# Two-layer graph network: slot rows of the convolutions go from one SBUF tile straight into another, in three parts of sources, with 14 slots per pair

## The chip, the cores and the metric

The kernel runs on one core of a Trainium2 chip. The metric is the device time of one execution in microseconds (us). The kernel before took 7372.2 us in the median of 9 runs (7339.61 to 7401.35). A profile is one more execution, taken by the hardware profiler: TensorE (PE, with its weight loads PEld), VectorE (DVE), ScalarE (ACT), GpSimd (POOL), and the DMA queues that SyncE (SP) and POOL issue on.

## The reference, cut to what matters

A graph of 12500 nodes with 128 features and 200000 edges, sorted by destination. First an attention layer over the edges, then three graph convolutions with a batch norm after each. The change touches the convolutions only (and the sorted lists that are made for them):

```python
def _gcn_conv(x, W, b, src, dst, norm, num_nodes):
    h = x @ W
    msg = h[src] * norm[:, None]
    out = jax.ops.segment_sum(msg, dst, num_segments=num_nodes)
    return out + b
...
h = _gcn_conv(x, W1, b1, src, dst, norm, n)
h = _batch_norm(jax.nn.relu(h), g1, beta1)
h = _gcn_conv(h, W2, b2, src, dst, norm, n)
h = _batch_norm(jax.nn.relu(h), g2, beta2)
h = _gcn_conv(h, W3, b3, src, dst, norm, n)
return _batch_norm(h, g3, beta3)
```

So each convolution adds, for every edge, the 128 floats of the source's row onto the destination's row.

## The kernel before

**Tiles and pairs.** Destinations are cut into 106 tiles of 118 nodes (`TN`, `NTT`), sources into 98 groups of 128 nodes (`NS`). A pair is one tile and one group. For each pair the kernel keeps `SB` = 13 slots, each with one edge; edges beyond those go to a list of up to `OV` = 768 per tile. The lists are made while the attention layer runs (`place_edges`): `dlS` holds each slot's destination within its tile, `gi_d` each slot's source within its group, `srcO` the rows of the listed edges.

**A convolution** (`conv_slots`, run three times) holds all source rows in SBUF (`hs`) and works in 12 blocks (`NBK`) of 9 tiles (`TB`).

- `take(b, m)` makes the rows of all slots of a block. For seven batches of 14 groups it loads the slots' sources (`gi`, SP's queue), compares them with the partition number on VectorE (`go`, L1221), multiplies that one-hot matrix by the group's rows on TensorE (`gp`, L1224), copies the result to `stage` on ScalarE (L1226) and writes it to a DRAM tile `m` (L1228).
- `reduce(b, m)` adds a block's rows up, tile by tile. It reads the tile's 1274 slot rows back from `m` (`mr`, L1245, three transfers per tile), gathers the 768 listed rows with six indirect transfers on POOL (`rows`, L148), makes the one-hot matrix of the destinations on VectorE (`oh`, L1249, 16 x 118 columns in one instruction) and runs on TensorE one matmul for the tile's own rows (L1159), ten over `mr` (L1253) and six over `rows` (L1255), all into one PSUM tile `zp`. Every matmul is float32 and appears as two instructions.
- `finish` closes a group of three tiles: it loads `tg` and `db` ahead of their matmuls, multiplies by `db` (L1163) and hands over to `use1`, `use2` or `use3`.

The reduction of block b-1 is written between the batches of `take(b)`:

```python
for g, _ in enumerate(take(b, taken)):
    while done < g * TB * SG // (NS - SG):
        next(tiles, None)
        done += 1
```

Each engine runs its instructions in the order in which the scheduler of the language put them, and SP and POOL issue their transfers in such an order too. Buffers: `stage` 2, `mr` 3, `rows` (pool `ga`) 5, `gi` 3, `m` 3 in DRAM.

Of the kernel before, what the change touches and what calls it, by code (L numbers as in the profile page):

```python
# [8 lines left out]
FP = mybir.dt.float32  # L9
# [8 lines left out]
P = 128  # L18
# [19 lines left out]
SB = 13  # L38
OV = 768
JO = OV // P  # L40
TB = P // SB
GN = 3
SG = 14
# [5 lines left out]
def tile_gnn(ctx: ExitStack, tc: tile.TileContext, x, src, dst, ea, wqkvT, weT, w1, w2, w3, par, out):  # L49
# [20 lines left out]
    assert TB % GN == 0  # L70
    RC = -(-SL // P)
    LP, LR = divmod(SL, RC)
    assert NS % SG == 0 and 112 < LP < P and LR and RC * P <= WE and NS * P * P < LATE and TN < P
    NBK = -(-NTT // TB)

    def groups(n, g):
        return [(a, min(g, n - a)) for a in range(0, n, g)]

# [15 lines left out]
    gi_d = dram.tile([NBK, NS // SG, TB, SG * SB], U8, name="gi_d")  # L94
# [563 lines left out]
    def fast():  # L658
# [6 lines left out]
        srcO = fc.tile([P, NTT, JO], I32, name="srcO")  # L665
        pars = fc.tile([P, 12], FP, name="pars")
# [12 lines left out]

        def place_edges(rt, ps):  # L680
# [10 lines left out]
            def turned(a, n, o, copy):  # L691

                av = a[:, :n * P].rearrange("t (p c) -> t c p", c=n)
                for c, m in groups(n, 4):
                    tp = ps.tile([P, 4, P], FP, name="et_p")
                    for i in range(m):
                        nc.tensor.transpose(tp[:, i, :NTT], av[:, c + i, :], ident[:NTT, :NTT])
                    copy(o[:, :, c:c + m].rearrange("p t c -> p c t"), tp[:, :m, :NTT])
# [102 lines left out]
            turned(x1, JO, dlS[:, :, RC:], nc.scalar.copy)  # L801
# [8 lines left out]
            turned(y1, JO, srcO, nc.vector.tensor_copy)  # L810
# [34 lines left out]
            for b in range(10, -1, -1):  # L845
# [7 lines left out]
                if sh < SL:  # L853
# [10 lines left out]
            nc.vector.tensor_scalar(mov, cur, P - 1, None, op0=ALU.bitwise_and)  # L864
            yield
            nc.vector.tensor_copy(A[turn][:, :SL].rearrange("t (k s) -> t k s", s=NS),
                                  mov.rearrange("t (s k) -> t k s", k=SB))
            turned(A[turn], RC, dlS[:, :, :RC], nc.scalar.copy)
# [5 lines left out]
            for b in range(NBK):  # L874
                tn = min(TB, NTT - b * TB)
                nc.sync.dma_start(gi_d[b, :, :tn, :].rearrange("g t k -> t g k"),
                                  sl[b * TB:b * TB + tn, :].rearrange("t (g k) -> t g k", g=NS // SG))
            if NTT % TB:
                none = rt.tile([NS // SG, (TB - NTT % TB) * SG * SB], U8, name="none")
                yield  # L880
                nc.vector.memset(none, 255)
                nc.sync.dma_start(gi_d[NBK - 1, :, NTT % TB:, :].rearrange("g t k -> g (t k)"), none)

# [266 lines left out]
        def finish(wk, table, t0, n, zp, use, ps, add):  # L1150

            tg = wk.tile([TN, GN, D], FP, name="tg")
            for a, b in ((0, 112), (112, TN)):
                nc.sync.dma_start(tg[a:b, :n, :], rows118(table, t0, n, a, b))
            db = wk.tile([P, GN * TN], FP, name="db")
            nc.sync.dma_start(db[:, :n * TN],
                              dinv_d[t0 * TN:(t0 + n) * TN].unsqueeze(0).to_broadcast([P, n * TN]))
            for i in range(n):
                nc.tensor.matmul(zp[:, i, :], tg[:, i, :], ident[:TN, :TN], start=True, stop=False)  # L1159
                add(i)  # L1160
                yield
# [5 lines left out]
        def conv_rows(table, use):  # L1167

            with ExitStack() as s:
# [8 lines left out]
                for t0, n in groups(NTT, GN):  # L1178
                    zp = ps.tile([P, GN, TN], FP, name="zp")

                    def add(i):
# [7 lines left out]

                    for _ in finish(wk, table, t0, n, zp, use, ps, add):  # L1190
                        pass

        def conv_slots(table, use):
# [3 lines left out]
            with ExitStack() as s:  # L1197
                tb = s.enter_context(tc.tile_pool(name="tb", bufs=1, space=PSUM))
                nums = tb.tile([P, TN], FP, name="nums")
                nc.vector.tensor_copy(nums, iota_f[:, :TN])  # L1200
                blocks = s.enter_context(tc.tile_pool(name="blocks", bufs=3, space=DRAM))
                gy = s.enter_context(tc.tile_pool(name="gy", bufs=3))
                gx = s.enter_context(tc.tile_pool(name="gx", bufs=3))
                sg = s.enter_context(tc.tile_pool(name="sg", bufs=2))
                mt = s.enter_context(tc.tile_pool(name="mt", bufs=3))
                ga = s.enter_context(tc.tile_pool(name="ga", bufs=5))
                wk = s.enter_context(tc.tile_pool(name="wk", bufs=2))
                ps = s.enter_context(tc.tile_pool(name="ps", bufs=2, space=PSUM))
                TS = TB * SB

                def take(b, m):
                    for g in range(NS // SG):
                        stage = sg.tile([TS, SG, D], FP, name="stage")
                        gi = gy.tile([P, TB, SG * SB], U8, name="gi")
                        nc.sync.dma_start(gi.rearrange("p t k -> p (t k)"),
                                          gi_d[b, g].rearrange("t k -> (t k)").unsqueeze(0)
                                          .to_broadcast([P, TS * SG]))
                        gv = gi.rearrange("p t (s k) -> p s t k", k=SB)
                        for a, n in groups(SG, 4):
                            go = gx.tile([P, 4, TB, SB], FP, name="go")  # L1220
                            nc.vector.tensor_scalar(go[:, :n], gv[:, a:a + n], iota_q, None, op0=ALU.is_equal)  # L1221
                            gp = ps.tile([TS, 4, D], FP, name="gp")
                            for i in range(n):
                                nc.tensor.matmul(gp[:, i, :], go[:, i].rearrange("p t k -> p (t k)"),  # L1224
                                                 hs[:, g * SG + a + i, :], start=True, stop=True)
                            nc.scalar.copy(stage[:, a:a + n, :], gp[:, :n, :])  # L1226
                        for x, y in ((0, 112), (112, TS)):
                            nc.sync.dma_start(m[x:y, g * SG:(g + 1) * SG, :], stage[x:y])  # L1228
                        yield

                def reduce(b, m):
                    for t0 in range(b * TB, min(NTT, (b + 1) * TB), GN):
                        n = min(GN, NTT - t0)
                        zp = ps.tile([P, GN, TN], FP, name="zp")

                        def add(i):
                            t = t0 + i
                            rows = ga.tile([P, JO, D], FP, name="rows")
                            for j in range(JO):
                                gather(rows[:, j, :], table, srcO[:, t, j:j + 1])  # L1240
                            k = (t - b * TB) * SB
                            mv = m[k:k + SB].rearrange("k s d -> (k s) d")
                            mr = mt.tile([P, RC, D], FP, name="mr")
                            for x, y, r in ((0, 112, RC), (112, LP, RC), (LP, LP + 1, LR)):
                                nc.sync.dma_start(mr[x:y, :r], mv[x * RC:(y - 1) * RC + r]  # L1245
                                                  .rearrange("(p c) d -> p c d", c=r))
                            oh = wk.tile([P, RC + JO, TN], FP, name="oh")
                            sh = list(oh.shape)
                            nc.vector.tensor_tensor(oh, nums.unsqueeze(1).to_broadcast(sh),  # L1249
                                                    dlS[:, t, :].unsqueeze(2).to_broadcast(sh), op=ALU.is_equal)  # L1250
                            for j in range(RC):
                                q = LP + (j < LR)
                                nc.tensor.matmul(zp[:, i, :], mr[:q, j, :], oh[:q, j, :], start=False, stop=False)  # L1253
                            for j in range(JO):
                                nc.tensor.matmul(zp[:, i, :], rows[:, j, :], oh[:, RC + j, :], start=False,  # L1255
                                                 stop=(j == JO - 1))

                        yield from finish(wk, table, t0, n, zp, use, ps, add)

                taken = None  # L1260
                for b in range(NBK + 1):
                    tiles = reduce(b - 1, taken) if b else iter(())
                    if b < NBK:
                        taken = blocks.tile([TS, NS, D], FP, name="m")
                        done = 0
                        for g, _ in enumerate(take(b, taken)):
                            while done < g * TB * SG // (NS - SG):
                                next(tiles, None)
                                done += 1
                    for _ in tiles:  # L1270
                        pass
# [178 lines left out]
```

## Time and profile before

| | us |
|---|---|
| median of 9 runs | 7372.2 |
| the profiled execution | 7425.4 |
| its span, first to last instruction | 7423.6 |
| attention layer and everything ahead of the convolutions, about | 3180 |
| first, second and third convolution, about | 1380, 1360, 1345 |
| the three stretches after them (batch norm, next rows, output), about | 60, 45, 54 |

The page gives busy times of the engines over the whole span: PE 4741.7, DVE 3409.4, ACT 1014.6, POOL 4011.6. These mix the attention layer with the convolutions, so the answers for a stretch of the span are of more use here. A matmul's duration is longer than the step from one to the next, since they are pipelined; steps are read from runs of equal instructions ("x20").

### The profile page before, as it was taken

Reading aid. Unit: us, or ns where it says so; the run is one execution under the profiler, and the core shown is the slowest. Engines: PE = TensorE matmul, PEld = TensorE weight load, DVE = VectorE, ACT = ScalarE, POOL = GpSimd, SP = SyncE. Lnnn points to the kernel's source line nnn. Section 1 sums busy time; section 2 is a strip of 40 time slices with the busy share of each in tenths; the row PEclk is TensorE's granted clock in tenths of the full one; section 3 lists DMA queues with packets and bytes.
Section 4 is the critical chain, followed back from the end, with each engine's and each line's share of the span. In section 5 each row is a group of like instructions: output and inputs, shape, how many; then the busy total and the mean of one; then the engine's idle time right before and its main releaser. Section 6 shows DMA issues by size and latency. Waiting matters only on the chain. (4 is left out here: it accounts for less than half of the span.)

```text
span 7423.6 us, 80384 instructions
## 1 busy us (share of the span) xinstructions
PE 4741.7 (64%) x28564; PEld 4380.5 (59%) x28564; DVE 3409.4 (46%) x5972; ACT 1014.6 (14%) x2374; POOL 4011.6 (54%) x3617
## 2 busy tenths in 40 slices
PE   5656666566666666647666667666666656666666
PEld 2555555555556555546665666566666656666666
DVE  6445688888557765523322234222222233233234
ACT  2111111101011111111111110111111111111110
POOL 1556688888767877624444443344444424444443
PEclk8667766666767676678877888777777777777777
DMA  5444444434444444366665666565666646566666
GB/s 173 117 118 119 120 109 109 108 107 112 114 109 113 111 120 121 97 157 177 163 164 156 161 161 170 155 161 150 159 160 162 159 139 168 157 163 160 155 159 172
DMA packets 607714, 1051.07 MB, mean 142 GB/s; under 512 B 191227, under 2 KB 418491, under 8 KB 607201
## 3 DMA queue, kind: packets, MB, share of 16 engines
q1 hardware_dynamic: 464311, 695.85, 34.1%
q0 software_dynamic: 142608, 348.39, 19.5%
q8 instruction: 232, 3.80, 0.2%
q14 instruction: 175, 1.43, 0.1%
q10 hardware_dynamic: 388, 1.60, 0.1%
HBM read 773.19 MB, written 272.26 MB: 141 GB/s over the span
## 5 line engine op out<-in xcount | busy, mean ns | idle before, releaser
L148 POOL DMA_INDIRECT rows<-t_d,srcO x1908 | 1820.7, 954 | 2378.9 <-PE zp L1159 671.6
L148 POOL DMA_INDIRECT kv<-kv_d,srcA x1696 | 2186.6, 1289 | 816.3 <-issue 488.0
L1224 PE MATMUL gp<-hs,go 128*117 128x128 f32 x7056 | 1072.1, 311 | 754.1 <-issue 552.4
L1224 PEld LDWEIGHTS gp<-hs,go 128*117 128x117 f32 x7056 | 970.8, 210 | 841.9 <-issue 664.6
L1253 PE MATMUL zp<-oh,mr 128*128 128x118 f32 x6360 | 1065.6, 339 | 624.0 <-DMA mr<-m 330.7
L1253 PEld LDWEIGHTS zp<-oh,mr 128*128 128x128 f32 x6360 | 1023.9, 253 | 644.0 <-issue 338.4
L1249 DVE TENSOR_TENSOR oh<-nums,dlS 128x1888 f32<-128x1888 f32 x318 | 674.1, 2121 | 1493.7 <-PE zp L1255 1415.9
L1019 PE MATMUL qe<-qt,oht 128*128 128x128 f32 x3392 | 841.4, 413 | 191.2 <-issue 80.0
L1019 PEld LDWEIGHTS qe<-qt,oht 128*128 128x128 f32 x3392 | 769.7, 311 | 233.2 <-issue 130.9
L1221 DVE TENSOR_SCALAR go<-gi,iota_q 128x468 f32<-128x468 uint8 x1008 | 434.1, 456 | 998.0 <-remote 455.3
L1226 ACT COPY stage<-gp 117x512 f32<-117x512 f32 x1008 | 523.2, 532 | 2297.7 <-PE gp L1224 863.9
L1089 PE MATMUL acc<-vals,oh 128*118 128x137 f32 x3392 | 547.1, 329 | 248.7 <-DVE vals L1082 163.3
L1089 PEld LDWEIGHTS acc<-vals,oh 128*118 128x118 f32 x3392 | 524.6, 225 | 273.9 <-DVE vals L1082 181.4
L1255 PE MATMUL zp<-oh,rows 128*128 128x118 f32 x3816 | 524.7, 288 | 36.8 <-issue 34.8
L1255 PEld LDWEIGHTS zp<-oh,rows 128*128 128x128 f32 x3816 | 497.3, 206 | 46.2 <-issue 46.1
L1020 DVE TENSOR_TENSOR kv<-qe,kv 128x512 f32<-128x512 f32 x424 | 287.9, 683 | 494.1 <-DMA kv<-kv_d,srcA 255.5
L1082 DVE TENSOR_TENSOR vals<-kv,vals 128x2048 f32<-128x2048 f32 x106 | 242.5, 2288 | 108.6 <-ACT vals L1081 78.1
L677 DVE TENSOR_TENSOR oh<-iota_f,dlA 128x1888 f32<-128x1888 f32 x106 | 224.2, 2115 | 132.5 <-PE qe L1019 55.1
L1058 PE MATMUL ends<-ident,mg 128*8 128x128 f32 x212 | 54.0, 344 | 352.6 <-DVE mg L1053 276.2
L1023 DVE TENSOR_REDUCE sc<-kv 128x128 f32<-128x2048 f32 x106 | 240.8, 2272 | 0.0
L1058 PEld LDWEIGHTS ends<-ident,mg 128*8 128x8 f32 x212 | 12.0, 96 | 371.5 <-DVE mg L1053 271.9
L1036 PE MATMUL sm<-wbd,et 128*128 128x32 f32 x848 | 169.3, 354 | 79.7 <-DVE mg L1075 55.6
(242 smaller groups left out, 3699.6 us busy)
## 6 DMA issues: line engine op xcount, KB each, us to landing
m<-stage SPq DMA_DIRECT2D x252, 784.0 KB
mr<-m SPq DMA_DIRECT2D x318, 560.0 KB
dw_b<-dlb_d SPq DMA_DIRECT2D x106, 512.0 KB
gi<-gi_d SPq DMA_DIRECT2D x252, 204.8 KB
rows<-t_d,srcO POOLq DMA_INDIRECT x1908
kv<-kv_d,srcA POOLq DMA_INDIRECT x1696
ebx<-in_edge_attr_dram SPq DMA_DIRECT2D x106, 256.0 KB
mr<-m SPq DMA_DIRECT2D x318, 75.0 KB
```

What stands on the lines that cost most here:

```text
L148: nc.gpsimd.indirect_dma_start(out=o, out_offset=None, in_=table[:, :], in_offset=bass.IndirectOffsetOnAxis(ap=idx, axis=0))
L1019: nc.tensor.matmul(qe[:, k, :], ohv[:, :, j + k], qt, start=True, stop=True)
L1020: nc.vector.tensor_tensor(qk[:, j:j + 4, :], qe, qk[:, j:j + 4, :], op=ALU.mult)
L1023: nc.vector.tensor_reduce(sc.rearrange("p h j -> p j h"), qk.rearrange("p j (h c) -> p j h c", h=H), AX.X, ALU.add)
L1082: nc.vector.tensor_tensor(vh[:, :, :, :C], kv[:, :, D:].rearrange("p j (h c) -> p j h c", h=H), vh[:, :, :, C:].to_broadcast([P, JJ, H, C] ...
L1089: nc.tensor.matmul(acc, oh[:, j, :], va[:, j, :], start=(j == 0), stop=(j == JJ - 1))
L1221: nc.vector.tensor_scalar(go[:, :n], gv[:, a:a + n], iota_q, None, op0=ALU.is_equal)
L1224: nc.tensor.matmul(gp[:, i, :], go[:, i].rearrange("p t k -> p (t k)"), hs[:, g * SG + a + i, :], start=True, stop=True)
L1226: nc.scalar.copy(stage[:, a:a + n, :], gp[:, :n, :])
L1249: nc.vector.tensor_tensor(oh, nums.unsqueeze(1).to_broadcast(sh), dlS[:, t, :].unsqueeze(2).to_broadcast(sh), op=ALU.is_equal)
L1253: nc.tensor.matmul(zp[:, i, :], mr[:q, j, :], oh[:q, j, :], start=False, stop=False)
L1255: nc.tensor.matmul(zp[:, i, :], rows[:, j, :], oh[:, RC + j, :], start=False, stop=(j == JO - 1))
```

## The change

The slot rows no longer pass through DRAM. The sources are cut into three parts, `PARTS = ((0, 5, 9), (45, 5, 9), (90, 1, 8))`: from group 0, nine pieces of five groups; from group 45, nine pieces of five; from group 90, eight pieces of one. For each block and part, `take` fills a tile `mr` in SBUF that holds all nine tiles' rows: piece q, slot k, tile t goes to partition 9k + q (8k + q in the third part) at column block t. That is one transfer from SBUF to SBUF per piece (L1259: 14 x 9 runs of 2560 bytes, or of 512 in the third part). Then `add` runs over the nine tiles of one part with five matmuls a tile (parts one and two) or, in the third, the own rows, one `mr` chunk and the listed rows. The third part's `add` also closes the groups of three tiles, so `zp` stays open over three parts. The part's `add` is written between the batches of the next part's `take`, the third's between those of the next block's first.

There are now 14 slots per pair, `OV` is 704 (the sixth gather of a tile has 64 rows), `rows` has 3 buffers and `stage` 2, `mr` 2, and `gi` 4; a batch is at most ten groups and its `gi` is loaded three batches ahead.

```diff
-SB = 13
-OV = 768
-JO = OV // P
+SB = 14
+OV = 704
+JO = -(-OV // P)
 TB = P // SB
+TS = TB * SB
-SG = 14
+PARTS = ((0, 5, 9), (45, 5, 9), (90, 1, 8))
...
+        nc.vector.memset(dlS, -1.0)
...
-            for b in range(NBK):
-                tn = min(TB, NTT - b * TB)
-                nc.sync.dma_start(gi_d[b, :, :tn, :].rearrange("g t k -> t g k"),
-                                  sl[b * TB:b * TB + tn, :].rearrange("t (g k) -> t g k", g=NS // SG))
...
+            for x in sum(batches, []):
+                s0, n, gi = batch(*x)
+                nc.sync.dma_start(gi[:NTT], sl[:, s0 * SB:(s0 + n) * SB])
+                if NTT % TB:
+                    nc.sync.dma_start(gi[NTT:], none[:, :n * SB])
...
+                def take(b, part, mr):
+                    _, n, pieces = PARTS[part]
+                    rows = mr[:pieces * SB, :, :n, :].rearrange("(k q) t c d -> q k t c d", k=SB)
+                    for _, q, m in batches[part]:
+                        s0, w, _ = batch(part, q, m)
+                        k = every.index((b, part, q, m))
+                        load_slots(k + 3)
+                        gv = gis[k][:, :TS * w].rearrange("p (t s k) -> p s k t", t=TB, k=SB)
+                        stage = sg.tile([TS, MB, D], FP, name="stage")
+                        for a, c in groups(w, 4):
+                            go = gx.tile([P, 4, SB, TB], FP, name="go")
...
+                            nc.scalar.copy(stage[:, a:a + c, :], gp[:, :c, :])
+                        for i in range(m):
+                            nc.sync.dma_start(rows[q + i], stage[:, i * n:(i + 1) * n, :])
                         yield
...
+                            if last:
+                                rows = ga.tile([P, JO, D], FP, name="rows")
+                                for j, (_, r) in enumerate(over):
+                                    gather(rows[:r, j, :], table, srcO[:r, t, j:j + 1])
+                                nc.tensor.matmul(zp, tg[:, t - t0, :], ident[:TN, :TN], start=False, stop=False)
+                            for j in range(w):
+                                nc.tensor.matmul(zp, mr[:K, t % TB, j, :], oh[:K, j, :], start=False, stop=False)
+                            for j, (_, r) in enumerate(over if last else []):
+                                nc.tensor.matmul(zp, rows[:r, j, :], oh[:r, w + j, :], start=False,
+                                                 stop=(j == JO - 1 and t == t0 + n - 1))
+                            yield
+                        if last:
+                            finish(wk, t0, n, zps.pop(t0), use, ph)
...
+                for b in range(NBK):
+                    for part in range(len(PARTS)):
+                        mr = mt.tile([P, TB, MC, D], FP, name="mr")
+                        done = 0
+                        for g, _ in enumerate(take(b, part, mr)):
+                            while done < g * TB // (len(batches[part]) - 1):
+                                next(tiles, None)
+                                done += 1
+                        for _ in tiles:
+                            pass
+                        tiles = add(b, part, mr)
```

## The prediction

> **What bounds the kernel now.** I read the page's slices first (attention layer to about 3180 us, then three alike stretches), and then the busy times by stretch, for the second and third convolution:
>
> ```profile
> core 0: us, PE busy (x) PEld busy (x) DVE busy (x) ACT busy (x) POOL busy (x), PEclk, DMA share, GB/s
> 4620.00:5980.00 1360.00, 885.51 (x5940) 851.26 (x5941) 392.32 (x511) 194.64 (x371) 605.55 (x636) 0.75 0.60 156
> 6025.00:7370.00 1345.00, 881.72 (x5956) 847.09 (x5955) 393.81 (x521) 195.05 (x373) 604.64 (x635) 0.76 0.61 158
> ```
>
> No engine is full. PE is busy for 65% and at a granted clock of 0.75; POOL for 45%; the DMA engines for 60%. A convolution of 12 blocks takes about 1360 us, 113 us a block of nine tiles. Something waits in a ring. The waits between 4700 and 5900 us, first SP's queue, then the engines (us in total, times, longest):
>
> ```profile
> SPq L1228 <- ACT stage L1226: 637.5, 49, 19.9
> SPq L1245 <- DMA mr<-m: 86.2, 36, 4.1
> ```
>
> ```profile
> POOL rows L148 <- PE zp L1159: 233.8, 28, 10.1
> ...
> PE zp L1253 <- DMA mr<-m: 104.2, 15, 8.1
> ```
>
> SP stands for half of the stretch at the store of `stage`, and behind it in the same queue wait the reads of `mr`, which TensorE then waits for. The timeline shows one turn of that ring (start, duration, in brackets the idle time before and its releaser):
>
> ```profile
> 5035.40 13.21 SPq L1228 DMA_DIRECT2D m<-stage  x6
> ...
> 5048.65 3.11 SPq L1245 DMA_DIRECT2D mr<-m  x5
> ...
> 5054.71 4.59 PE L1253 MATMUL zp<-oh,mr 128*128 128x118 f32 x20 [7.22 <-DMA mr<-m]
> ...
> 5061.06 2.40 PE L1253 MATMUL zp<-oh,mr 128*128 128x118 f32 x20
> 5061.27 0.94 POOL L148 DMA_INDIRECT rows<-t_d,srcO  x1 [9.71 <-PE zp L1159]
> 5062.52 0.95 POOL L148 DMA_INDIRECT rows<-t_d,srcO  x1 [0.30 <-issue]
> ```
>
> The reads go out when the stores have, PE resumes about 6 us after the first and 3 us after the last of five issues, and its first twenty matmuls run at half speed (4.59 us) and the next at full speed (2.40, 0.12 us each). POOL, free since long, gets a buffer back only now. Its own step is 0.94 + 0.30 = 1.247 us a gather, 7.48 us a tile of six, 67.3 us of the 113 us block.
>
> **What the change removes.** The block's trip through DRAM: per block 5.87 MB written and 5.87 MB read, 7 x 2 stores and 9 x 3 loads on SP. In their place come 26 transfers within SBUF (6.32 MB). SP issues 49 transfers a block where it issued 57, at about 0.34 us each: 17 us, hidden. Moved bytes fall from about 17.8 to 12.2 MB a block (1.6 for `gi`, 3.2 for the gathers, 1.1 for `tg` and `db` stay). At 156 GB/s with 0.60 busy an engine moves 16.3 GB/s while busy, so the new block needs 28 us of each of 14 engines for its rows and 23 us for the rest: not the bound by itself.
>
> **What PE, DVE and ACT do then.** A tile has 18 matmuls instead of 17, in pairs; with the block's 98 gather-by-matmul pairs that is 520 instructions, 62 us at 0.12 us. DVE has 98 x 126 columns of `go` (468 took 0.456 us: 12 us) and 17 x 118 columns of `oh` a tile (1888 took 2.12 us: 20 us), under 40 us a block with the rest; ACT's copies about 17 us. All are below POOL's 67 us. So POOL's gathers are what is late next, and the question is whether they run without a break.
>
> **They do not.** All of a tile's gathers now belong to the third part, with three buffers for nine tiles. After the last tile of a block POOL fetches three tiles of the next one (22.4 us) and stops until the next block's first third-part tile has been added. In between PE must do parts one and two. In the built program's order the instructions from the last `add` of a block to the first of the next are 54 `gp` pairs, 90 `mr` pairs and 8 of that tile: 304 x 0.12 = 36.5 us. To this come transfers that PE cannot hide. The second part's rows may not be written before the last `add` has freed their tile; with two `stage` buffers the five batches then go through in three rounds: batches one and two at once, the third when the first has landed, the fifth when the third has. I take 3.5 us a landing (the 560 KB reads above: 3 to 6 us; these are 315 KB, so 2 to 6) and find PE waiting about 7 us, most of it for the fifth batch. The last tile itself: 2.5 us for its gather to land (2 to 4, same rows) and 16 matmuls at half speed, 0.23 us each, 3.7 us. POOL's pause is 36.5 + 7 + 2.5 + 3.7 - 22.4 = 27 us, and the block 94 us.
>
> A convolution: 106 x 7.48 = 793 us of gathers, eleven pauses of 27 us, one longer pause in the first block (33 us; 68 in the first convolution, where the first `gp` matmul started 35 us after the first gather), 8 us of tail: 1131 us, 1166 in the first, together 3428 against 4085 before.
>
> The sixth gather of a tile has 64 rows. The trace has none of that size: it costs between as much as the others and half of their 0.94 us; net of the shorter lead, 0 to 35 us a convolution. I take the middle, 53 us in all.
>
> **Edits ahead of the convolutions.** Slot lists get 1372 columns for 1274: the groups at L848 to L854 (55 us) grow by 4 us; three copies and a memset replace one copy; 14 list stores replace 12, with the loads of the next tiles behind them on SP. VectorE is busy 2104 of these 3180 us and POOL with its steps 2700, so this can be hidden: 0 to 15 us (only work is added), I take 8. The `gi` load three batches ahead is worth nothing of its own: it hides behind 20 us of PE, and without that cover it would cost a landing of some 3 us a batch.
>
> Sum: 7425.4 - (4085 - 3428) - 53 + 8 = 6723 for a run like the profiled one, which lay 0.7% above the median (7372.2 / 7425.4 = 0.993): 6675 us.
>
> **A rule weighed against the trace: how many engines a transfer uses.** The row first:
>
> ```profile
> L159 ACTq DMA_DIRECT2D dr<-in_dst_dram x1: 569/569/569, 0.8 to 0.8; - x1
> L164 DVE CAST df<-dr x1: 981/981/981, 13.2 to 13.2; 125x1600 f32<-125x1600 int32 x1
> ```
>
> 781 KB in 125 rows, issued at 0.8 and used at 13.2 us: 63 GB/s, what four engines move at 16.3. So the count of rows can keep a transfer to a few engines, and the new transfers have 14 rows of 9 runs against 126 rows. The Trainium skill ("DMA: Bandwidth & Descriptors", section on why a DMA increments its semaphore by 16) lets a transfer use the largest number up to 16 that divides the outer counts of both sides: 5 for those 125 rows, 14 here. By it the rows take the 28 us above. The same page's rules for authors speak against the change: transfers should be merged towards 1 MiB, and 784 KB ones become 315 and 63 KB. By its fit (2 us and bytes at 436 GB/s) an estimate for 315 KB is 2.7 us a landing, which would shorten each block by about 2 us.
>
> **Rivals.** (A) The forecast, POOL's gathers with a pause of about 27 us. For it speaks the steady 0.30 us between gathers whenever a buffer is free. If PE hides every landing and steps at 0.113 us (the bare pitch within x20 runs), and the short gather costs half, the pause is 18 us and the time 6310.
>
> (B) The three rounds decide more than the gathers. PE's 885 us for 5940 instructions in the stretch above are 0.149 us each; with that and landings of 4 us the stretch from last to first `add` is 45.3 + 8.5 = 54 us instead of 43.5, the pause 38 us, the time 7040; at 0.149 and 6 us it ends near 7300, where hardly anything is gained. For it: the half clock after each wait, and waits that are now put in series on two `stage` buffers. Against it: between the rounds PE has other work queued.
>
> (C) Slower: the row transfers run on few engines. 6.32 MB at 16.3 GB/s are 388 us of engine time a block; on k engines with 23 us of other traffic a block takes 388/k + 23 us. That passes the present 113 us at k = 4 (120 us, about 7600 us in all); at 2 it is 217 us a block and over 11000 us. For it: the 125-row row. Against it: the 5-row tails of the stores before ran beside the large ones without a wait of their own.
>
> (D) The change does not do what it says: with more listed edges than 704 in some tile the program would take its other branch, which gathers every edge (16 gathers a tile, over 2100 us of POOL a convolution). Counting the given inputs, the fullest tile has 645 beyond 14 per pair, so I give it nothing.
>
> **How the numbers follow.** A 0.71; B 0.17, of which 0.02 ends within 0.5% of now and 0.02 above; C 0.08; still lower than A's lower bound 0.04. A difference of 0.5% is about what a measurement of this kernel can tell from none. Faster: 0.71 + 0.13 + 0.04 = 0.88; same 0.02; slower 0.10. The range runs from A's bound, 6310, to B's value, 7040, and leaves out about 0.2.
>
> **What would show it.** Right: POOL's gathers in the convolutions at 1.25 us steps with one pause of 20 to 35 us a block, released by a third-part matmul; SP's long waits on that same matmul, no longer on `stage`; block period 90 to 97 us; PE's clock low in the third part. Wrong: a pause over 40 us with PE waiting on `mr<-stage` (B); a busy share of the DMA engines with few of them at work and rows landing after 10 us or more (C); gathers that never pause, so that something else sets 94 us; or a sixth gather much dearer or cheaper than 0.5 to 0.94 us.

## The result and the profile after

The changed kernel is slower: 8030.1 us in the median of 10 runs (8012.7 to 8065.7) against 7380.1 us of the kernel before beside it, a ratio of 1.089 (95% interval 1.087 to 1.092). The forecast was 6675, in a range from 6310 to 7040. The profiled execution has a span of 8010.0 us; its convolutions take about 1570, 1557 and 1559 us, where 1380, 1360 and 1345 were read before, and a block takes 131 us.

One fact has to be told first, since no later number can be read without it: the runs came from several chips, and they are of two kinds. The same kernel before takes 7264 to 7401 us on the one kind (all the runs above are of it) and 6161 to 6166 us on the other. Every ratio below is to the kernel before on the same chip, and that time stands beside it. I call the first kind chips with the hold, for the reason that the profile shows. No chip came up in two of the sets of runs below, so what I call a kind of chip may as well be a state that a chip was in.

The second and third convolution of the changed kernel, by the windows of its profile:

```profile
core 0: us, PE busy (x) PEld busy (x) DVE busy (x) ACT busy (x) POOL busy (x), PEclk, DMA share, GB/s
4788.00:6345.00 1557.00, 1014.12 (x6201) 928.48 (x6201) 501.81 (x770) 197.12 (x419) 601.59 (x636) 0.73 0.34 94
6386.00:7945.00 1559.00, 1011.98 (x6181) 925.53 (x6181) 501.31 (x768) 196.52 (x418) 602.76 (x636) 0.73 0.34 94
```

The DMA engines went from 0.60 busy to 0.34, as the change should make them, POOL's busy time is the same, and each convolution is 200 us longer. No engine is near to full; only VectorE's share rose, from 0.29 to 0.32. The waits between 4900 and 6200 us, the engines first, then SP's queue:

```profile
POOL rows L153 <- PE zp L1294: 640.6, 38, 45.4
ACT stage L1257 <- remote: 373.2, 50, 17.9
...
DVE go L1252 <- remote: 166.4, 36, 7.8
...
DVE oh L1284 <- remote: 126.0, 13, 14.4
```

```profile
SPq L1259 <- ACT stage L1257: 585.7, 126, 31.8
```

POOL waits for TensorE's third part 640 us out of 1300, where the forecast had one pause of 27 us a block. SP's long wait for `stage` has not gone, and ScalarE and VectorE wait for "remote": the profile finds no instruction of this core whose end released them. The timeline shows POOL's three pauses of one block and, between them, what "remote" hides:

```profile
5526.83 0.96 POOL L153 DMA_INDIRECT rows<-t_d,srcO  x1 [45.30 <-PE zp L1294]
...
5539.28 2.98 PE L1255 MATMUL gp<-hs,go 128*126 128x128 f32 x12 [0.65 <-issue]
...
5544.64 0.37 ACT L1257 COPY stage<-gp 126x256 f32<-126x256 f32 x1 [4.93 <-remote]
5545.07 1.35 PE L1255 MATMUL gp<-hs,go 128*126 128x128 f32 x8 [2.81 <-ACT stage L1257]
...
5552.70 1.07 ACT L1257 COPY stage<-gp 126x512 f32<-126x512 f32 x2 [7.69 <-remote]
...
5560.34 0.96 POOL L153 DMA_INDIRECT rows<-t_d,srcO  x1 [11.43 <-PE zp L1294]
...
5591.77 0.95 POOL L153 DMA_INDIRECT rows<-t_d,srcO  x1 [9.05 <-PE zp L1294]
```

From 5526.83 to 5549 us POOL issues 18 gathers without a break. TensorE ends two groups of `gp` at 5542.3 and 5546.4; ScalarE, idle, copies them only at 5552.70, over three microseconds after the last gather of the run. In a stretch of 22 us of gathers TensorE issues 54 matmuls; in 40 us without, 255:

```profile
5486.00:5526.00 40.00, 35.61 (x255) 34.38 (x255) 21.98 (x35) 7.75 (x18) 0.00 (x0) 0.85 0.29 82
5562.00:5584.00 22.00, 9.06 (x54) 7.88 (x53) 4.31 (x6) 1.54 (x3) 15.85 (x17) 0.75 0.34 90
```

Counted over the second convolution by the time since a run of gathers began, TensorE issues 6.2 matmuls per us in the first 6 us of a run, then 2.0 to 2.2 up to 16 us, and 1.0 from 16 to 24 us; 5.0 where no gather runs. Its semaphore is raised 2.5 times per us without gathers and 0.2 times from 16 to 24 us into a run. ScalarE's copies that start more than 8 us into a run start 7.0 us (median) after the last matmul that they need has ended; outside of runs it is 0.08 us. (The profile models the ends of matmuls, so it does not tell whether a matmul itself ends late or only its count is seen late; I speak of late counts.) So a block is 67 us of gathers and 64 us of pauses in which TensorE does most of its work: 131 us. The two hardly overlap.

### The profile page after: what moved, and what is told of

It reads as the page before. It is cut to its first block, busy times and chain, and to the rows that moved or that the text cites. A ratio compares the mean times of both kernels' runs of the same rounds, so it can differ in the third digit from the quotient of the medians.

```text
span 8010.0 us, 83647 instructions
## 1 busy us (share of the span) xinstructions
PE 5134.3 (64%) x29309; PEld 4617.2 (58%) x29309; DVE 3749.4 (47%) x6759; ACT 1027.7 (13%) x2518; POOL 4024.5 (50%) x3617
## 5 line engine op out<-in xcount | busy, mean ns | idle before, releaser
L1255 PE MATMUL gp<-hs,go 128*126 128x128 f32 x7056 | 1172.6, 324 | 890.6 <-issue 419.6
L1255 PEld LDWEIGHTS gp<-hs,go 128*126 128x126 f32 x7056 | 1041.1, 228 | 1116.8 <-ACT stage L1257 537.1
L1292 PE MATMUL zp<-oh,mr 126*128 126x118 f32 x6996 | 1149.3, 322 | 524.5 <-DVE oh L1284 250.9
L1284 DVE TENSOR_TENSOR oh<-nums,dlS 128x590 f32<-128x590 f32 (+1 forms) x954 | 812.8, 853 | 1302.0 <-remote 492.1
L1292 PEld LDWEIGHTS zp<-oh,mr 126*128 126x128 f32 x6996 | 1063.6, 235 | 590.4 <-DVE oh L1284 289.0
L1252 DVE TENSOR_SCALAR go<-gi,iota_q 128x504 f32<-128x504 uint8 (+2 forms) x1152 | 631.9, 569 | 1161.1 <-remote 600.7
L1257 ACT COPY stage<-gp 126x512 f32<-126x512 f32 (+2 forms) x1152 | 535.9, 486 | 3197.6 <-PE gp L1255 1336.0
L1294 PE MATMUL zp<-oh,rows 128*128 128x118 f32 x3816 | 672.8, 326 | 17.2 <-DMA rows<-t_d,srcO 13.7
L1294 PEld LDWEIGHTS zp<-oh,rows 128*128 128x128 f32 x3816 | 597.6, 232 | 66.6 <-issue 22.9
L1182 DVE TENSOR_TENSOR zt<-zp,db 128x354 f32<-128x354 f32 x108 | 55.9, 517 | 418.9 <-remote 276.9
```

What stands on the lines that cost most here:

```text
L1252: nc.vector.tensor_scalar(go[:, :c], gv[:, a:a + c], iota_q, None, op0=ALU.is_equal)
L1255: nc.tensor.matmul(gp[:, i, :], go[:, i].rearrange("p k t -> p (k t)"), hs[:, s0 + a + i, :], start=True, stop=True)
L1257: nc.scalar.copy(stage[:, a:a + c, :], gp[:, :c, :])
L1284: nc.vector.tensor_tensor(oh[:, :sh[1]], nums.unsqueeze(1).to_broadcast(sh), dl.unsqueeze(2).to_broadcast(sh), op=ALU.is_equal)
L1292: nc.tensor.matmul(zp, mr[:K, t % TB, j, :], oh[:K, j, :], start=False, stop=False)
L1294: nc.tensor.matmul(zp, rows[:r, j, :], oh[:r, w + j, :], start=False, stop=(j == JO - 1 and t == t0 + n - 1))
```

## The experiments

The theories. **G**: while POOL issues indirect gathers, TensorE's semaphore counts reach the other engines late; what is already queued goes on for some 4 to 6 us, then TensorE nearly stops. **W**, the prediction's rival B: the rounds of row transfers on two `stage` buffers. **T**: the gathers' bytes and descriptors crowd the DMA engines. **N**: each gather costs TensorE the same time wherever it stands. **M**: the kernel before is held by its trip through DRAM, as the prediction read it. **D** and **H**: a short break between gathers lifts the hold, or does not.

### The gathers away, or replaced (a chip with the hold; before 7295 us)

The first kernel leaves out the convolutions' gathers; the listed chunks multiply a constant tile.

```diff
-                                rows = ga.tile([P, JO, D], FP, name="rows")
-                                for j, (_, r) in enumerate(over):
-                                    gather(rows[:r, j, :], table, srcO[:r, t, j:j + 1])
+                                rows = still
```

> The changed kernel without the listed rows' gathers: the six matmuls per tile read one zeroed tile, so the listed edges are left out of the sums. Theory G (in a long run of gathers on POOL, TensorE's semaphore counts arrive late and it nearly stops; block = 67 us of gathers + 64 us of PE): a block falls from 131.5 to 65-75 us, a convolution to about 900, the time to 5900-6150 us. Theory W (my rival B: three rounds of row transfers decide the 44 us pause, gathers have no part in it): parts one and two keep 44 + 22 = 66 us and part three needs 28 us of PE, so a block takes 94 us or more and the time is 6700-6900 us.

6082.7 us, a ratio of 0.834 (0.830 to 0.838). The rounds of row transfers are still all there, so W is wrong as the main cause; the second convolution takes 906 us, 75 us a block, and the clock is back (the row has 881 us of it):

```profile
4160.00:5041.00 881.00, 799.36 (x6081) 749.52 (x6082) 490.66 (x759) 195.21 (x416) 0.00 (x0) 0.93 0.41 121
```

The next keeps the bytes: one plain load of a tile's 768 rows on SP.

```diff
-                                for j, (_, r) in enumerate(over):
-                                    gather(rows[:r, j, :], table, srcO[:r, t, j:j + 1])
+                                nc.sync.dma_start(rows, table[t * TN % 8192:t * TN % 8192 + JO * P, :].rearrange("(j p) d -> p j d", p=P))
```

> The changed kernel with the six gathers of a tile replaced by one plain load on SP's queue of as many bytes in the same 512-byte runs (rows in order instead of the listed ones, so wrong edges are summed). Theory G: POOL issues nothing, so nearly as without gathers, 5950-6350 us. Theory T (the gathers' traffic on the DMA engines, not POOL's issuing, delays the rest): within 3% of the changed kernel, 7800-8200 us. Theory W: 6700-6900 us.

6274.1 us, 0.860 (0.856 to 0.865): T is wrong. Then the same number of transfers on POOL's queue, but plain ones:

```diff
-                                    gather(rows[:r, j, :], table, srcO[:r, t, j:j + 1])
+                                    a = (t * 97 + j * P) % 8192
+                                    nc.gpsimd.dma_start(rows[:r, j, :], table[a:a + r, :])
```

> The changed kernel with each gather replaced by a plain load of as many rows, issued on the same POOL queue one by one (wrong rows are summed). If every transfer that POOL issues holds TensorE's counts (G, general): 7600-8100 us. If only the indirect form does (G, narrow): 6000-6500 us. Theory T: 7800-8200 us.

6123.6 us, 0.840 (0.834 to 0.845). And the same number of gathers with 16 rows each; the other rows of the list are left out:

```diff
-                over = groups(OV, P)
+                over = [(a, 16) for a, _ in groups(OV, P)]
```

> The changed kernel with as many gathers, each of 16 rows instead of 128 (or 64), the matmuls on them likewise 16 rows deep (most listed edges are left out). G by instruction: each gather holds TensorE as before if POOL's step stays near 1.25 us, 7600-8100 us. G by rows, or T by bytes: TensorE runs on, 6000-6600 us; POOL's duration of a gather tells what a row costs.

7954.4 us, 1.091 (1.085 to 1.097), no faster than with 128 rows. The gathers' groups of these two kernels (columns: count, busy time, mean ns, idle time before and its releasers):

```profile
L1290 POOL DMA_DIRECT2D rows<-t_d x1908 | 1054.9, 560 | 1920.3 <-PE zp L1295 1712.8 <-DMA rows<-t_d 88.0 <-issue 37.2
```

```profile
L153 POOL DMA_INDIRECT rows<-t_d,srcO x1908 | 1615.1, 846 | 3213.5 <-PE zp L1294 2350.1 <-issue 519.3 <-remote 162.4
```

So the hold belongs to the indirect instruction itself, 846 ns with an eighth of the rows; neither rows, bytes nor POOL's queue make it. The waits agree: in the three kernels without indirect gathers nothing between 4300 and 5500 us is put down to "remote"; with gathers of 16 rows it is 725 us between 4700 and 5900 us, summed over the engines.

### Gathers spread over the parts, and halved (a chip without the hold; before 6161 us)

Two of a tile's six gathers go into each part's `add`, with two, later nine and three, buffers of two chunks (`LW` = 2).

```diff
+                            rows = ga.tile([P, LW, D], FP, name="rows")
+                            mine = list(enumerate(over))[part * LW:(part + 1) * LW]
+                            for i, (j, (_, r)) in enumerate(mine):
+                                gather(rows[:r, i, :], table, srcO[:r, t, j:j + 1])
...
-                                rows = ga.tile([P, JO, D], FP, name="rows")
-                                for j, (_, r) in enumerate(over):
-                                    gather(rows[:r, j, :], table, srcO[:r, t, j:j + 1])
```

> The changed kernel with two of a tile's six gathers in each of the three parts' adds, two buffers of two chunks for them; nothing is left out. G (a long run of gathers keeps TensorE's counts from the other engines; the first 4 to 6 us of a run are free): runs are now two gathers, 2.5 us, paced by the adds, so nearly all of TensorE's work goes on beside them, and the block comes near to the 77 us that it has without gathers: 6100 to 6700 us. N (every gather costs TensorE its 1 us wherever it stands): 7900 to 8150, as the changed kernel.

7035.3 us, 1.142 (1.140 to 1.144).

> The same with nine buffers of two chunks, so that nothing paces the gathers within a part. G: POOL runs ahead and fetches a part's 18 chunks in one run of 22 us, three times a block; 22 less 5 us, three times, stand in TensorE's way as before: 7400 to 8000 us. N: 7900 to 8150. A theory in which the pacing has no part (more buffers only help) gives no more than the kernel with two buffers.

6121.0 us, 0.9935 (0.992 to 0.995). Both expectations failed, since they took the hold for granted and this chip hasn't got it: in the kernel with nine buffers TensorE issues 6.7 to 8.8 matmuls per us up to 24 us into a run of gathers, and no engine waits for "remote". What is left is POOL's wait for buffers, in the waits between 4400 and 5600 us, first with two buffers, then with nine (with two, TensorE also waits 181 us for the gathered rows):

```profile
POOL rows L156 <- PE zp L1302: 400.9, 104, 22.6
```

```profile
POOL rows L156 <- PE zp L1302: 159.7, 79, 10.9
```

The next halves the gathers: three a tile, which the last three chunks read once more.

```diff
-                                for j, (_, r) in enumerate(over):
+                                for j, (_, r) in enumerate(over[:JO // 2]):
...
-                                nc.tensor.matmul(zp, rows[:r, j, :], oh[:r, w + j, :], start=False,
+                                nc.tensor.matmul(zp, rows[:r, j % (JO // 2), :], oh[:r, w + j, :], start=False,
```

> The changed kernel with three gathers a tile in place of six; the last three chunks read the first three again. G: runs are nine gathers, 11.2 us, of which 5 are free: three runs with 6 us each on top of the 77 us of a block without gathers, 36 blocks: 6600 to 6900 us. N: half of the 1948 us that leaving out all of them saved: 6950 to 7150. A POOL queue that is the bound by its own 67 us a block gives 6083, as without any, since 34 us hide.

6027.0 us, 0.978 (0.976 to 0.979), with 75 us a block, as many as in the changed kernel without any gather: without the hold, half of POOL's 67 us hides behind TensorE altogether. Last, the kernel before without its gathers, which read a constant tile:

```diff
-                            rows = ga.tile([P, JO, D], FP, name="rows")
-                            for j in range(JO):
-                                gather(rows[:, j, :], table, srcO[:, t, j:j + 1])
+                            rows = still
```

> The kernel before without the convolutions' gathers; the listed chunks read one constant tile. G: the kernel before too pays for its runs of six gathers (7.5 us, of which 4 are free), some 3.5 us nine times a block, so without them its 113 us block shrinks to some 80 to 85 us: 6200 to 6500 us. M (its block is set by the trip through DRAM, the stores and reads on SP's queue): 7100 to 7350.

6086.9 us, 0.987 (0.985 to 0.988). It says nothing of G here, but it does bear on M: with the whole trip through DRAM the kernel before needs only 80 us a block. Once more, again on a chip without the hold:

> The kernel before without the convolutions' gathers, once more. Where the kernel before takes 7260 to 7400 us: if its 113 us a block are the gathers' hold on TensorE's counts (G), it falls to 6080 to 6250 us, a ratio of 0.83 to 0.85; if they are the trip through DRAM and SP's queue (M, the prediction's reading), it stays at 7000 to 7350. Where it takes 6160: 0.987 again under both.

6080.4 us beside 6164, 0.987 (0.985 to 0.988). On a chip with the hold this kernel was not run.

### The changed kernel and the spread one, once more (a chip with the hold; before 7264 us)

> The changed kernel once more, beside the kernel before. Where the kernel before takes 7300 to 7400 us, every theory says 1.09 of it, 7950 to 8050. Where it takes 6160 us, as it did beside the last four kernels: G there has no grip (in those traces TensorE issued over 8 instructions a microsecond in runs of gathers of 6 to 16 us), so the changed kernel is left with its 67 us of gathers and one pause a block: the prediction's block of 94 us and 3000 us ahead, 6300 to 6550 us, a ratio of 1.02 to 1.07. If the loss were in the change's order of work and not in the gathers' hold on TensorE, the ratio stays at 1.09: 6650 to 6800 us.

7897.9 us, 1.089 (1.086 to 1.093): the loss repeats on another chip of this kind.

> The kernel with two gathers in each part and nine buffers of two chunks, once more. Where the kernel before takes 6160 us: 6100 to 6140 again. Where it takes 7300 to 7400: G says runs of 18 and more gathers, three times a block, 7400 to 8000 us; a hold on TensorE that goes by the gathers' number alone says 7900 to 8050; no hold at all says 6100 to 6250.

7165.0 us, 0.987 (0.984 to 0.991), faster than G's 7400 to 8000. The same number of gathers as in the changed kernel (1.089 on this chip), spread, so N with its 7900 to 8050 is wrong. The hold slows TensorE so much that POOL has to wait for it, and its runs are six gathers long in the median, not 18; in those that last longer, TensorE falls to some 2 matmuls per us after 8 us. G's mechanism stands, my run lengths did not.

### A short break after every two gathers (before 6161 us, then 7401)

A memset of each chunk on POOL goes ahead of its gather; the built order is two memsets, two gathers, two memsets. In the trace the gap after every second gather grows from 0.30 to 0.53 us by it, less than I had taken.

```diff
+                                    nc.gpsimd.memset(rows[:, j, :], 0.0)
                                     gather(rows[:r, j, :], table, srcO[:r, t, j:j + 1])
```

These and a spread kernel with three buffers ran on a chip without the hold.

> The changed kernel with a memset of each chunk on POOL ahead of its gather; the built order is two memsets, two gathers, two memsets and so on, some 0.8 us more for each pair, so a block's 54 gathers take about 89 us of POOL in place of 67; nothing is left out. Where the kernel before takes 7260 to 7380 us: if a short gap lets TensorE's counts through (D), its work goes on beside the gathers, and the block is 89 us and a pause of some 25: 7300 to 7500 us. If the gaps do nothing (H), 89 and 64 us: 8600 to 8900. Where the kernel before takes 6160 us, 6900 to 7150 under either.

6820.4 us, 1.107 (1.104 to 1.109): a block of 101 us, 76 of gathers and 25 of pause.

> Two gathers in each part and nine buffers, with the same memsets ahead of the gathers. Where the kernel before takes 7260 to 7380 us: D gives a block of 90 to 98 us, the gathers' 89 being the longest, 6450 to 6750 us; H gives 107 and 20 us more, 7600 to 7900. Where it takes 6160: 6350 to 6600.

6100.5 us, 0.991 (0.988 to 0.994).

> The kernel before with the same memsets ahead of its gathers. Where the kernel before takes 7260 to 7380 us: D lets TensorE go on, the block falls from 113 us to 90 to 100, 6400 to 6850 us; H adds 22 us a block, 7900 to 8150. Where it takes 6160: 6250 to 6500.

6167.6 us, 1.002 (1.001 to 1.003).

> Two gathers in each part with three buffers of two chunks, between the kernels with two and with nine. Where the kernel before takes 7260 to 7380 us: G says that shorter runs hold TensorE less but that POOL then waits for it more: 6800 to 7300 against 7165 with nine buffers. Where it takes 6160: 6300 to 6700, between the 7035 of two buffers and the 6121 of nine.

6563.4 us, 1.066 (1.064 to 1.068), between two and nine buffers as expected.

D against H stays untold by these. All three with memsets came out below what I had expected without the hold, the spread one by 250 us or more, since the memsets cost less than I had taken. But the kernel before with memsets is, within 0.2%, the kernel before on such a chip, and its profile is the one look at its block there:

```profile
4100.00:5036.00 936.00, 736.21 (x5647) 716.77 (x5647) 370.84 (x495) 190.17 (x367) 690.46 (x1176) 0.88 0.84 216
```

The row has 936 us of the second convolution, which takes 984 us in all, 82 us a block, with the trip through DRAM at 216 GB/s and the DMA engines 0.84 busy. SP's waits between 4150 and 5000 us have the same first line as the profile that the prediction was built on:

```profile
SPq L1228 <- ACT stage L1226: 421.0, 72, 9.3
```

Half of SP's time stands there on this chip too. The line was never a price.

### The changed kernel without the hold (before 6166 us)

> The changed kernel, beside the kernel before. Where the kernel before takes 6160 us there is no hold on TensorE's counts, and the prediction's block should stand: 67 us of gathers and one pause of 25 to 27 us, 92 to 96 us, with 3000 us ahead 6450 to 6600 us, a ratio of 1.05 to 1.07. Where it takes 7260 to 7380: 1.09 again, with pauses of 64 us a block.

6622.0 us, 1.074 (1.072 to 1.076), a little above the expected 6450 to 6600. Here the prediction's block is found, beside a kernel before that is faster than it:

```profile
4245.00:5380.00 1135.00, 925.60 (x6201) 839.73 (x6201) 506.36 (x779) 198.61 (x421) 606.60 (x635) 0.84 0.47 129
5420.00:6560.00 1140.00, 932.60 (x6201) 844.19 (x6201) 503.30 (x771) 198.27 (x420) 609.05 (x635) 0.83 0.46 128
```

```profile
4749.12 0.96 POOL L153 DMA_INDIRECT rows<-t_d,srcO  x1 [0.31 <-PE zp L1275]
4781.97 0.95 POOL L153 DMA_INDIRECT rows<-t_d,srcO  x1 [25.48 <-PE zp L1294]
```

```profile
4704.00:4726.00 22.00, 18.27 (x104) 15.76 (x104) 8.65 (x15) 3.48 (x8) 16.73 (x18) 0.77 0.58 156
```

All 54 gathers of a block run through at the step of 1.25 us, then one pause of 25.48 us (20 to 28 us in the others after a convolution's first), released by a third-part matmul; block to block 91 to 96 us. In 22 us of gathers TensorE issues 104 matmuls, where the same row with the hold had 54 in as long, and no wait is put down to "remote".

The spread kernel with memsets ran beside it, and then once more on another chip:

> Two gathers in each part, nine buffers, and a memset of each chunk on POOL ahead of its gather. Where the kernel before takes 6160 us: 6100 again. Where it takes 7260 to 7380: D (a short break between two gathers and the next two lets TensorE's counts through) 6450 to 6750; H (it does not; only the gathers' number and their time count) 7600 to 7900, against 7165 without the memsets.

6107.7 us, 0.992 (0.989 to 0.994).

> Two gathers in each part, nine buffers, and a memset of each chunk on POOL ahead of its gather, once more. Where the kernel before takes 6160 us: 6100. Where it takes 7260 to 7380: D (a short break after every two gathers lets TensorE's counts through) 6450 to 6750 us; H (it does not; the gathers' number and time count) 7600 to 7900; without the memsets it was 7165.

This one had it, before 7401: 7242.9 us, 0.978 (0.974 to 0.982). Both D (6450 to 6750) and H (7600 to 7900) missed. The hold is there in spite of the breaks, in the waits between 4600 and 5800 us:

```profile
ACT stage L1264 <- remote: 156.8, 15, 21.2
DVE oh L1291 <- remote: 117.1, 26, 5.6
```

A break of 0.53 us after two gathers does not lift it (a longer one was not tried); it costs nothing that shows either, because POOL waits for TensorE anyway (305 us between 4600 and 5800 us), and that H had wrong. This version is faster than both kernels on either kind of chip, than the kernel before by 0.8 to 0.9% and by 2.2%. The changed kernel's slots in SBUF are sound; its order of gathers was not.

## Why the prediction was wrong

The step that failed is the overlap. In both kernels I let TensorE work beside POOL's gathers at full pace, at no cost and without a reason; on the chips where the forecast was measured the two hardly overlap.

**The bound before: wrong, by that step.** I read SP's wait at the store of `stage` and PE's for `mr<-m` as a ring through DRAM that sets 113 us, and took POOL's 67 us as hidden work. The kernel before does the same ring in 82 us a block on a chip without the hold, and 6087 against 6161 us without any gather there. On the chips where it takes 7264 to 7401 us, the extra is bound up with the gathers: leaving them out takes the changed kernel from 1.089 of the kernel before to 0.834, and replacing them by plain transfers to 0.840. On those chips the kernel before was not run without its gathers, but its trace shows the same hold: in its second convolution TensorE issues 7.5 matmuls per us in the first 4 us of a run of gathers and 2.0 from 6 to 16 us, and ScalarE's copies that start more than 8 us into a run start 6.9 us (median) after their matmuls have ended. In the kernel before with memsets on a chip without the hold, these are 8.5, 6.6 and 0.04 us. How much of the 31 us between 113 and 82 us a block is the hold is not shown. The sign stood in the waits of before, between 4700 and 5900 us, in lines that I passed over because each was smaller than SP's:

```profile
ACT stage L1226 <- remote: 187.5, 55, 6.5
DVE go L1221 <- remote: 151.9, 52, 6.6
DVE oh L1249 <- remote: 6.7, 1, 6.7
DVE zt L1163 <- remote: 3.5, 1, 3.5
POOL rows L148 <- remote: 3.0, 4, 2.1
```

They add up to 353 us, over engines that may wait at the same time, in a stretch of 1200. SP waited for ScalarE, and ScalarE for counts of TensorE that came late. The same sum is 699 us in the changed kernel (4900 to 6100 us) and nothing in every run without the hold that I summed.

**What is late next: right in kind.** POOL's gathers at 1.25 us, 67.3 us a block, released by a third-part matmul: as written.

**The pause: right without the hold, 64 us with it.** The term that failed there is the 22.4 us of gathers that were taken off 36.5 us of TensorE's work at 0.12 us a matmul. With the hold little goes on beside the three tiles, so the subtracted 22.4 us all but fall away (45 us measured where 27 were forecast); and the rest of the third part, put beside gathers at no cost, makes two more pauses of 9 to 11 us. Without the hold: 20 to 28 us against 27, block 91 to 96 against 94, convolution 1135 and 1140 against 1131.

**The sum.** On a chip without the hold the kernel took 6622 us, near the 6675 on record, but that is luck: the first gather of the first convolution comes at 3004 us and not at about 3180, the 0.7% (48 us) taken off for a slow profile has no place there, and the steps after the first gather are longer. By the prediction's terms from 3004 it would be about 6540 (3004 + 3428 + 159 for the three stretches between and after - 53). Of the 80 us between, 40 are the short gather: 64 rows take 0.903 us against 0.944, 0.04 us off the step, 4 us a convolution, and not the 17 that I took. Another 30 are the pause in the first block of the later two convolutions (49 and 48 us against 33). The rest I did not trace.

**Rivals.** B expected waits in the transfers' rounds; its pause of over 40 us came, and for another reason. C is refuted: the semaphore of a transfer issued at 5486.60 was updated once at 5487.82 us and 14 times more up to 5489.84 us, 3.2 us after the issue. That agrees with the rule of the Trainium skill ("DMA: Bandwidth & Descriptors", section on why a DMA increments its semaphore by 16) as I applied it, 14 engines. The same page's fit, which stands there for transfers that GpSimd issues, gave an estimate of 2.7 us. The edits ahead cost nothing that shows: the first `gp` matmul comes at 3187 us, before at 3224.

**The sign.** It would be slower even where the mechanism is all as forecast: 94 us against the 82 that the kernel before needs without the hold, some 430 us over 36 blocks, 456 measured (6622.0 less 6166.0). There the kernel before spreads its 54 gathers over the whole block and hides all but about 2 of the 67 us (82 us a block against 80 without gathers); the change puts them into the part that closes a block, and a pause behind them. With the hold the loss is 650 us.

## What to carry to other kernels

A long wait on an issuing queue says who came last, not what sets the pace: follow it back through each engine that it names, and add up the rows put down to "remote" before believing any ring. A transfer that hides behind other work hides only as long as it is spread over that work; count the buffers and where the issues stand, and not only the busy time. Where gathers and matmuls should overlap, look in the trace whether matmuls per microsecond stay the same while a run of gathers lasts, and time a change on more than one chip.

## What the runs showed of the hardware

- On some chips a run of indirect gathers on POOL delays TensorE's semaphore counts: 7.0 us (median) from the modelled end of the matmuls to the copy that waits for them, more than 8 us into a run; on others 0.08 us. Plain transfers on the same queue (560 ns each) had no such cost. What differs between the chips is open, and so is the path on which the counts are held.
- The cost goes with the instruction, not its rows: gathers of 16 rows take 846 ns and those of the changed kernel (128 rows, the sixth 64) 947 ns in the mean, at the same loss.
- The attention layer gathers too, and ends 100 to 150 us earlier on the chip without the hold (first `gp` matmul of the changed kernel at 3036 us, against 3142 and 3187 on two with it). How much of that is the hold was not tried.
- An SBUF-to-SBUF transfer of 14 x 9 runs of 2560 bytes takes SP 0.81 us to issue, not the 0.34 that I took from other transfers; it stayed hidden.
